# A graph network with attention on one core: the residual base moved behind a softmax, two bias rows loaded later, GpSimd given other operands in the first quad

## The chip, the core and the metric

One core of a Trainium2 chip runs the whole program. The metric is device microseconds of one execution; the time of a kernel is the median of its runs. Engines are named as the profile names them: PE (matmul), PEld (its weight loads), DVE (vector engine), ACT (scalar engine), POOL (GpSimd), SP (the engine that issues nearly all DMAs here).

## The reference

x is 1024 x 512. Sixteen graphs of 64 nodes share 16384 edges; each graph has 256 rows of conditions (`cond`, 16 x 256 x 512). All is float32.

```python
h = jnp.maximum(_layernorm(x, axis=-1), 0.0)
...
h = (h - mu) * rsqrt(var + EPS) * bn_w + bn_b
h = _gcn(h, src, dst, gcn_in_w, gcn_in_b, n)
for i in range(L):                                   # L = 4
    a = _attn(_ln(h, ln2_w[i], ln2_b[i]), cond, Wq[i], Wk[i], Wv[i], Wo[i])
    h = h + a
    u = _ln(h, ln3_w[i], ln3_b[i]) @ geglu_w[i] + geglu_b[i]
    val, gate = jnp.split(u, 2, axis=-1)
    f = val * jax.nn.gelu(gate, approximate=False)
    h = h + f @ ffo_w[i] + ffo_b[i]
h = _gcn(h, src, dst, gcn_out_w, gcn_out_b, n)
return h + x_in            # x_in is the relu above; x itself is added to the result
```

The attention has 8 heads of 64: 64 queries of a graph against its 256 conditions.

## The kernel before, in words

**Operands in parts.** [...] In the names, `ah`, `al`, `as` are the parts of a left operand, `bh`, `bl`, `bs` those of a right one, and `gr`, `gl` those of the first GEGLU weights.

**A layer.** After the queries a loop over g = 0 to 6 treats eight blocks of two graphs. In pass g PE makes keys and values of block g+1 (L370; ACT scales them out of PSUM at L381, ACT or DVE copy at L386 and L388), the scores of block g+1 (L831, in `scores`), and mixes block g (L865) and its output product (L903). DVE takes the maximum of the scores (L838), ACT the exponentials (L843), DVE the reciprocal and the scaling (L846, L848). `split_cond` splits the conditions of block g+2: high part `ah_c` on ACT (L318), low part `al_c` on DVE (L319), third part `as_c` on POOL (L324).

**The base.** What is added to the last GCN's result (x, its relu, and the bias row of the last GCN) is worked out a block of 128 rows at a time, two blocks in each layer: `fetch_x` loads x again in passes g = 1 and 2, `base_of` takes the relu on ACT (L1556), adds the bias row and the relu on DVE (L1558, L1559) and stores the sum (L1560). `load_row` (L136) loads a bias row into all 128 partitions: `bias_out` for the base, `ffb` for the feed-forward bias, which `add_bias` (L1568) adds to the rows from pass g = 6 on.

**The first GEGLU round** of a layer is written as four quads (L301 on PE), each a chain of products with sums on DVE between them (L982), the gelu on ACT (L972) and the product into `fT` (L1000, L1001). Between a quad's instructions `fill()` takes the next piece of the splitting of the seven right operands, in the order EARLY = 0, 1, 4, 6, 5, 3, 2. For an operand in BESIDE, `right_beside` has DVE make only the low halves (L1037) and POOL the third parts (L1039); for the others DVE makes both (`begin_right` L1017, `finish_right` L1025). POOL's sums for the later rounds' weights (L1081) come behind these in its order.

**Rounds 1 to 3** run as chunks (products at L1109, DVE sums at L1127 and L1144, third parts of the next chunk's weights on POOL at L1050). In the last chunk the splitting of the first rows of f (L318, L319, third part on POOL) comes in too. The output product (L1252) follows: `fr` are rows of f loaded back from DRAM (L1211), `wff` the output weights (L1220), split at L1226, L1229 and L1233.

**What sets the order.** Each engine and the SP queue take instructions in program order, which a scheduler fixes from the code's order and from contexts: `tc.issue_after(i)` places instructions behind instruction i in the order, `waiting_for(i, engine)` makes that engine's next instruction wait for i, and `in_order` and `pin` keep a given order. `scores.last` is the last scaling (L848) of the softmax that `scores` issued last.

Of the kernel before, what the change touches and what calls it, by code (L numbers as in the profile page):

```python
# [15 lines left out]
OP = mybir.AluOpType  # L16
# [5 lines left out]
TINY = 2.0 ** -12  # L22
# [4 lines left out]
def gnn_kernel(  # L27
# [26 lines left out]
    nc = tc.nc  # L54
    pin = tc.keep_in_program_order

    N, D = x.shape
# [7 lines left out]
    KC = D // P  # L65
# [4 lines left out]
    R = DFF // D  # L70
# [235 lines left out]
    def twelve_bits(t):  # L306
        return t.bitcast(F32R)
# [3 lines left out]

    def left_parts(x, name, t=None):

        parts = [slots_of(len(x), f"{n}_{name}") for n in ("ah", "al", "as")]
        for h, l, s, x in zip(*parts, x):
            nc.scalar.mul(twelve_bits(h), x, INWARD * TINY)  # L318
            nc.vector.scalar_tensor_tensor(twelve_bits(l), h, -1.0 / TINY, x, OP.mult, OP.add)  # L319
            if t:  # L320
                t.tensor_tensor(twelve_bits(s), h, l, OP.subtract)  # L321
                continue
            for k in range(2):
                nc.gpsimd.tensor_tensor(twelve_bits(s)[:, k, :], h[:, k, :], l[:, k, :],  # L324
                                        OP.subtract)
        return parts
# [678 lines left out]

    SPLIT = (0, 5, 6, 4, 1, 3, 2)
    EARLY = (0, 1, 4, 6, 5, 3, 2)
    BESIDE = (4, 6)

    def begin_right(name, x, h, s):  # L1010

# [189 lines left out]
    class Output:  # L1201
# [8 lines left out]
                self.raw[n] = slot(f"fr_{self.l}_{n}")  # L1210
                nc.sync.dma_start(self.raw[n], f_dram[s, 2 * u:2 * u + 2].rearrange("c p n -> p c n"))  # L1211

        def split(self, n, t=nc.vector):
            if n in self.raw:
                self.f[n] = left_parts([self.raw.pop(n)], f"f_{self.l}_{n}", t)

        def fetch_w(self, u):
            if u < UNITS:
# [206 lines left out]
    for l in range(L):  # L1425
# [119 lines left out]
        def fetch_x(nb):  # L1545
            if not fetched:
                fetched["bias"] = three_halves(f"bias_out_{l}")[:, :D]
                load_row(gcn_out_b, 0, "bias_out", fetched["bias"])
            fetched[nb] = acc_tile(f"x_again_{nb}")
            nc.sync.dma_start(fetched[nb], x[nb * P:(nb + 1) * P, :])  # L1550

        def base_of(nb):


            xt, bias_out, xn = fetched.pop(nb), fetched["bias"], acc_tile(f"again_{nb}")
            nc.scalar.activation(xn, xt, AF.Relu, bias=x_shift[:, nb:nb + 1],  # L1556
                                 scale=x_root[:, nb:nb + 1])
            nc.vector.tensor_tensor(xt, xt, bias_out, OP.add)  # L1558
            nc.vector.tensor_tensor(xt, xt, xn, OP.add)  # L1559
            nc.sync.dma_start(base_dram[nb], xt)  # L1560
# [2 lines left out]

        def add_bias(t, *blocks):
            if not ffb:
                ffb.append(load_row(ffo_b, l * D, f"ffb_{l}"))
            for nb in blocks:
                t.tensor_tensor(h[nb], h[nb], ffb[0], OP.add)  # L1568

# [11 lines left out]
        for g in range(NG - 1):  # L1581
# [36 lines left out]
                ln3_norm(g - 2, g - 1, behind=mix.last)  # L1618
                add_bias(nc.gpsimd, g - 2, g - 1)
            if g in (1, 2):  # L1620
                base_of(2 * l + g - 1)
            if l == 0:
                fetch_cond(g + 3)
            split_cond(l, g + 2)
# [125 lines left out]
                load()  # L1750
        sum_chunk(2)

        def split_rest(short):
            long = begin_split(0, False)
            next(long, None)
            with waiting_for(split_left.low, mybir.EngineType.Pool):
                for flow in short, long:
                    for _ in flow:
                        pass
# [4 lines left out]
        for r in range(1, R):  # L1764
            f = Gated(l, r)
            for c in range(KC):
                n = (r - R + 2) * KC + c
                if n == -1:
                    output.fetch_w(0)
                if (r, c) == (R - 1, KC - 2):  # L1770
                    output.fetch(0)
                chunk = ready.pop(0)
                flow = chunk.steps(lambda: before and sum_chunk(1))
                chunk.f = f
                next(flow)
                if 0 < n < 5:
                    next(ahead)
                for _ in islice(short, 2):
                    pass
                next(flow)  # L1780
                if before:
                    split_rest(short)
                    load()
                for _ in parts:
                    pass
                if (r, c) == (R - 1, KC - 1):
                    with in_order(mybir.EngineType.Activation), in_order(mybir.EngineType.DVE), \
                            in_order(mybir.EngineType.Pool):
                        output.split(0, nc.gpsimd)
                    output.fetch(1)  # L1790
                for step in range(3):
                    if before:
                        next(before, None)
                    next(flow)
                    if step == 1 and not before:
                        split_rest(iter(()))
                        load()
                before = flow
                short = begin_split(0, True)
                if n == 0:  # L1800
                    next(ahead)
# [153 lines left out]
```

## Time and profile before

| what | value |
|---|---|
| median of 3 runs | 2304.32 us (2302.94 to 2304.63) |
| the profiled execution | 2308.55 us |
| its span in the trace | 2306.8 us |
| PE busy | 2271.7 us, 98% |
| DVE, ACT, POOL busy | 1738.5 us (75%), 1169.6 us (51%), 750.3 us (33%) |
| granted TensorE clock, mean | 0.998 |

The rows of the timeline give the start in us, the duration in us, the engine, the line, the operation, and output<-inputs with their shapes; consecutive equal instructions are one row with a count (x4). In square brackets stands the idle time of that engine just before, and what ended it. The rows of the waits give engine, line, what was waited for, and then the total in us, the number of times, and the longest.

### The profile page before, as it was taken

The numbers are of one execution on the slowest core, as the hardware profiler recorded it, in microseconds if no ns is written. First come the engines' busy times: TensorE is split into PE (matmuls) and PEld (weight loads), VectorE is DVE, ScalarE is ACT, GpSimd is POOL, SyncE is SP. The second block draws the span as 40 slices with busy tenths as digits, with TensorE's granted clock in tenths as the row PEclk, the third lists the DMA queues.
The fourth block names the chain that finished last, engine by engine and source line by source line (L and its number), as shares of the span: only waits on it lengthen the run. The fifth ranks groups of instructions, "written<-read, shape, count | busy, mean of one in ns | idle before, by whom it ended". The sixth has DMA issues, their size and how long they took to land. (4 is left out here: it accounts for less than half of the span.)

```text
span 2306.8 us, 34462 instructions
## 1 busy us (share of the span) xinstructions
PE 2271.7 (98%) x12496; PEld 1757.1 (76%) x12496; DVE 1738.5 (75%) x3172; ACT 1169.6 (51%) x2245; POOL 750.3 (33%) x647
## 2 busy tenths in 40 slices
PE   8999999999999999999999999999999999999999
PEld 5677887587887888488787888578788788668777
DVE  9886556999986556989987554989988554899965
ACT  7555445465355445465356444556437444556521
POOL 1121213486022224377022222368112113168301
PEclk9999999999999999999999999999999999999999
DMA  7042211234512101133522111133531111043551
GB/s 214 2 151 70 69 62 36 82 119 146 183 46 74 47 28 37 60 122 96 209 91 74 38 38 38 38 109 101 192 137 51 41 47 46 1 128 110 183 171 59
DMA packets 144114, 204.42 MB, mean 89 GB/s; under 512 B 11241, under 2 KB 68913, under 8 KB 143937
## 3 DMA queue, kind: packets, MB, share of 16 engines
q1 hardware_dynamic: 141840, 196.72, 25.8%
q0 software_dynamic: 1376, 4.30, 0.6%
q8 instruction: 103, 1.69, 0.3%
q10 hardware_dynamic: 720, 1.11, 0.1%
q14 instruction: 75, 0.61, 0.1%
HBM read 151.75 MB, written 50.34 MB: 88 GB/s over the span
## 5 line engine op out<-in xcount | busy, mean ns | idle before, releaser
L324 POOL TENSOR_TENSOR as_c<-ah_c,al_c 128x512 fp32r<-128x512 f32 x128 | 200.4, 1595 | 906.6 <-DVE al_c L319 711.3
L1123 ACT ACTIVATE g<-g 128x512 f32<-128x512 f32 x192 | 112.4, 585 | 152.3 <-PE g L1109 150.7
L381 ACT ACTIVATE k<-k 128x512 f32<-128x512 f32 x125 | 73.0, 586 | 197.9 <-PE k L370 197.9
L1252 PE MATMUL fy<-bl_wff,al_f 128*128 128x512 f32 x512 | 160.1, 392 | 1.3 <-DVE bl_wff L1229 0.8
L318 ACT ACTIVATE ah_f<-fr 128x1024 fp32r<-128x1024 f32 x64 | 67.9, 1061 | 183.7 <-PE fy L1252 90.7
L1252 PE MATMUL fx<-bs_wff,as_f 128*128 128x512 f32 x512 | 160.4, 393 | 0.6 <-DVE as_f L321 0.6
L1252 PE MATMUL fy<-bh_wff,ah_f 128*128 128x512 f32 x512 | 158.4, 391 | 0.2 <-ACT ah_f L318 0.2
L386 DVE COPY kT<-k 128x512 f32<-128x512 f32 x54 | 37.2, 689 | 156.6 <-PE k L370 156.6
L370 PE MATMUL v<-bs_wv,as_c 128*128 128x512 f32 x508 | 137.4, 393 | 7.2 <-ACT v L381 7.2
L370 PE MATMUL v<-bh_wv,ah_c 128*128 128x512 f32 x508 | 141.2, 400 | 0.0
L1050 POOL TENSOR_TENSOR gsa<-gha,gla 128x512 fp32r<-128x512 f32 x96 | 124.2, 1315 | 40.2 <-DVE gla L1045 40.2
L843 ACT ACTIVATE pr<-sc,nmax 128x256 f32<-128x256 f32 x256 | 118.2, 476 | 37.3 <-DVE nmax L838 36.7
L370 PE MATMUL v<-bl_wv,al_c 128*128 128x512 f32 x508 | 136.4, 390 | 0.0
L370 PE MATMUL k<-ah_c,bh_wk 128*128 128x512 f32 x500 | 135.0, 392 | 0.0
L381 ACT ACTIVATE v<-v 128x512 f32<-128x512 f32 x127 | 75.2, 592 | 116.9 <-PE v L370 116.9
L370 PE MATMUL k<-as_c,bs_wk 128*128 128x512 f32 x500 | 132.1, 395 | 1.7 <-ACT k L381 1.7
L370 PE MATMUL k<-al_c,bl_wk 128*128 128x512 f32 x500 | 133.7, 389 | 0.0
L1109 PE MATMUL g<-gr,gha 128*128 128x512 f32 x384 | 120.0, 394 | 0.0
L1109 PE MATMUL g<-gr,gsa 128*128 128x512 f32 x384 | 120.0, 394 | 0.0
L1109 PE MATMUL g<-gl,gla 128*128 128x512 f32 x384 | 118.3, 389 | 0.0
L370 PEld LDWEIGHTS v<-bs_wv,as_c 128*128 128x128 f32 x508 | 93.1, 188 | 32.4 <-ACT v L381 10.3
L1252 PEld LDWEIGHTS fy<-bl_wff,al_f 128*128 128x128 f32 x512 | 96.3, 188 | 24.5 <-DVE bl_wff L1229 3.7
(321 smaller groups left out, 5820.7 us busy)
## 6 DMA issues: line engine op xcount, KB each, us to landing
f_dram<-fT SPq DMA_DIRECT2D x128, 256.0 KB, 2.1
fr<-f_dram SPq DMA_DIRECT2D x64, 512.0 KB, 4.3
ct<-cond_dram SPq DMA_DIRECT2D x48, 512.0 KB, 4.9
wff<-in_L_gnn_ffo_w_dram SPq DMA_DIRECT2D x32, 512.0 KB, 6.9
gxb<-in_L_gnn_geglu_w_dram SPq DMA_DIRECT2D x96, 128.0 KB, 2.5
gxa<-in_L_gnn_geglu_w_dram SPq DMA_DIRECT2D x96, 128.0 KB, 2.5
cond<-in_L_gnn_cond_dram SPq DMA_DIRECT2D x32, 256.0 KB, 3.8
cond_dram<-ct SPq DMA_DIRECT2D x16, 512.0 KB, 3.3
```

What stands on the lines that cost most here:

```text
L318: nc.scalar.mul(twelve_bits(h), x, INWARD * TINY)
L324: nc.gpsimd.tensor_tensor(twelve_bits(s)[:, k, :], h[:, k, :], l[:, k, :], OP.subtract)
L370: pin(nc.tensor.matmul(self.bank, twelve_bits(left[k // 2])[:, k % 2, self.c * P:(self.c + 1) * P], twelve_bits(right[k // 2])[:, k % 2, : ...
L381: nc.scalar.mul(self.bank, self.bank, 1.0 + TINY)
L386: nc.vector.tensor_copy(self.to(), self.bank)
L843: nc.scalar.activation(pr3[:, a, :], ps3[:, a, :], AF.Exp, bias=nmax[:, a:a + 1], accum_out=tot[:, a:a + 1])
L1050: split_left.last = pin(t.tensor_tensor(s_at, h_at, l_at, OP.subtract))
L1109: pin(nc.tensor.matmul(to, self.part(i, which)[:, k, :], self.rights[i][which].bitcast(F32R)[:, k, :], start=start and k == 0, stop=stop a ...
L1123: pin(nc.scalar.mul(to, to, 1.0 + TINY))
L1252: pin(nc.tensor.matmul(to, twelve_bits(left[which][0])[:, k, b * P:(b + 1) * P], twelve_bits(right[which])[:, k, :], start=u == 0 and whic ...
```

## The change

1. `base_of` is called under `tc.issue_after(scores.last.ins)`, so that it stands behind the softmax that was issued last.
2. The loads of `bias_out` and `ffb` wait on SP for `scores.last`, so they are made in the pass in which they are asked for.
3. BESIDE is (1, 4) in place of (4, 6).
4. In the last chunk of the last round, POOL's third parts of the weights wait for the low part of the first rows of f, and stand between it and its third part.

```diff
-    def left_parts(x, name, t=None):
+    def left_parts(x, name, t=None, between=None):
...
-            nc.vector.scalar_tensor_tensor(twelve_bits(l), h, -1.0 / TINY, x, OP.mult, OP.add)
+            left_parts.low = nc.vector.scalar_tensor_tensor(twelve_bits(l), h, -1.0 / TINY, x,
+                                                            OP.mult, OP.add)
+            if between:
+                between()
...
-    BESIDE = (4, 6)
+    BESIDE = (1, 4)
...
-                load_row(gcn_out_b, 0, "bias_out", fetched["bias"])
+                with waiting_for(scores.last, mybir.EngineType.SP):
+                    load_row(gcn_out_b, 0, "bias_out", fetched["bias"])
...
-                ffb.append(load_row(ffo_b, l * D, f"ffb_{l}"))
+                with waiting_for(scores.last, mybir.EngineType.SP):
+                    ffb.append(load_row(ffo_b, l * D, f"ffb_{l}"))
...
-                base_of(2 * l + g - 1)
+                with tc.issue_after(scores.last.ins):
+                    base_of(2 * l + g - 1)
...
-        def split_rest(short):
+        def split_rest(short, behind=None):
...
-            with waiting_for(split_left.low, mybir.EngineType.Pool):
+            with waiting_for(behind or split_left.low, mybir.EngineType.Pool):
...
                 if before:
-                    split_rest(short)
+                    if not the_last:
+                        split_rest(short)
                     load()
...
-                        output.split(0, nc.gpsimd)
+                        output.split(0, nc.gpsimd, lambda: split_rest(short, left_parts.low))
```

PE's order is the same in both kernels. Lines of the changed kernel stand 3 to 8 higher (L838 is L841, L1558 is L1562).

**The base on DVE, layer 1, pass g = 0.** `al_c_2` is the low part of block 2's conditions, `nmax_1` belongs to the softmax of block 1. Before:

```order
L319 SCALAR_TENSOR_TENSOR al_c_2_0_21145<-ah_c_2_0_21143,ct_2_0_20865 128x1024
L1558 TENSOR_TENSOR x_again_21226<-x_again_21226,bias_out_21224 128x512
L1559 TENSOR_TENSOR x_again_21226<-x_again_21226,again_21432 128x512
L319 SCALAR_TENSOR_TENSOR al_c_2_1_21146<-ah_c_2_1_21144,ct_2_1_20866 128x1024
L838 TENSOR_REDUCE nmax_1_0_21101<-sc_1_0_21081 128x2
L838 TENSOR_REDUCE nmax_1_1_21111<-sc_1_1_21082 128x2
L846 RECIPROCAL inv_1_0_21107<-tot_1_0_21104 128x2
```

After, the same place reads:

```order
L319 SCALAR_TENSOR_TENSOR al_c_2_0_21145<-ah_c_2_0_21143,ct_2_0_20865 128x1024
L319 SCALAR_TENSOR_TENSOR al_c_2_1_21146<-ah_c_2_1_21144,ct_2_1_20866 128x1024
L841 TENSOR_REDUCE nmax_1_0_21101<-sc_1_0_21081 128x2
L841 TENSOR_REDUCE nmax_1_1_21111<-sc_1_1_21082 128x2
L849 RECIPROCAL inv_1_0_21107<-tot_1_0_21104 128x2
```

The two additions are now in pass g = 1, behind the softmax of block 2:

```order
L851 TENSOR_SCALAR pr_2_3_21422<-pr_2_3_21422,inv_2_3_21426 128x256 x2
L895 SCALAR_TENSOR_TENSOR ol_1_21367<-oh_1_21366,po_1_21290 128x512
L1562 TENSOR_TENSOR x_again_21226<-x_again_21226,bias_out_21224 128x512
L896 TENSOR_TENSOR os_1_21368<-oh_1_21366,ol_1_21367 128x512
L1563 TENSOR_TENSOR x_again_21226<-x_again_21226,again_21432 128x512
L389 COPY v_2_0_21469<-v_2_1_21455 128x512
```

The second block's additions, which stood among the scalings of block 1's softmax, go behind the softmax of block 3 in the same way. On ACT the relu of the first block keeps its place; that of the second moves from the exponentials of block 1 to behind the last scaling of v in pass g = 1.

**The loads on SP, layer 0, passes g = 0 and 1.** `cond_0` to `cond_3` are raw conditions of block 3, `ct` are turned ones on their way to DRAM. Before:

```order
L1550 DMA x_again_16072<-in_x_dram 128x512
L1560 DMA base_dram<-x_again_16072 128x512
L1550 DMA x_again_16400<-in_x_dram 128x512
L270 DMA cond_0_15953<-in_L_gnn_cond_dram 128x512
L270 DMA cond_1_15954<-in_L_gnn_cond_dram 128x512
L270 DMA cond_2_15955<-in_L_gnn_cond_dram 128x512
L270 DMA cond_3_15956<-in_L_gnn_cond_dram 128x512
```

After:

```order
L1554 DMA x_again_16072<-in_x_dram 128x512
L136 DMA bias_out_16070<-in_L_gnn_gcn_out_b_dram 128x512
L270 DMA cond_0_15953<-in_L_gnn_cond_dram 128x512
L270 DMA cond_1_15954<-in_L_gnn_cond_dram 128x512
L270 DMA cond_2_15955<-in_L_gnn_cond_dram 128x512
L270 DMA cond_3_15956<-in_L_gnn_cond_dram 128x512
L276 DMA cond_dram<-ct_3_0_16040 128x1024
```

The bias row, which waits for block 1's softmax, now stands ahead of the four loads; the base's store and the second load of x have gone further down. Until now the rows of the next layer stood in the output product's start, here that of layer 0, with rows of layer 1's bias:

```order
L1193 DMA f_dram<-fT_3_1_19573 128x512 x2
L136 DMA bias_out_21224<-in_L_gnn_gcn_out_b_dram 128x512
L1211 DMA fr_1_19641<-f_dram 128x2x512
L1193 DMA f_dram<-fT_3_2_19664 128x512 x2
L1220 DMA wff_1_19704<-in_L_gnn_ffo_w_dram 128x2x512
L1220 DMA wff_2_19706<-in_L_gnn_ffo_w_dram 128x2x512
L136 DMA ffb_22720<-in_L_gnn_ffo_b_dram 128x512
L1211 DMA fr_2_19722<-f_dram 128x2x512
```

After, the two L136 rows are missing there; `bias_out` of layers 1 to 3 stands behind the loads of `ct_3`, and `ffb` ahead of the first GEGLU weights `wval` and `wgate`.

**DVE in the first quad and the start of the second, layer 0** (`gu`, `g` and `gd` with L982 are the quad's own sums, which PE waits for; `gt` is an aid of ACT's for a third part). Before:

```order
L1025 SCALAR_TENSOR_TENSOR gl_1_18319<-ln3T_0_1_17698,gr_1_18295 128x512
L982 TENSOR_TENSOR g_0_0_0_18313<-gd_0_0_18309,gu_0_0_0_18311 128x512
L1025 SCALAR_TENSOR_TENSOR gl_1_18319<-ln3T_0_1_17698,gr_1_18295 128x512
L982 TENSOR_TENSOR g_0_0_0_18312<-gc_0_0_18308,gu_0_0_0_18310 128x512
L1037 SCALAR_TENSOR_TENSOR gl_4_18331<-ln3S_0_17701,gr_4_18329 128x512
L982 TENSOR_TENSOR gd_0_0_18309<-gd_0_0_18309,gu_0_0_0_18310 128x512
L1000 SCALAR_TENSOR_TENSOR fT_0_0_18314<-ga_0_0_18125,gcols,g_0_0_0_18312 128x512
L1001 SCALAR_TENSOR_TENSOR fT_0_0_18314<-gd_0_0_18309,gcols,g_0_0_0_18313 128x512
L1037 SCALAR_TENSOR_TENSOR gl_4_18331<-ln3S_0_17701,gr_4_18329 128x512
L1037 SCALAR_TENSOR_TENSOR gl_6_18354<-ln3T_1_0_17699,gr_6_18352 128x512
L982 TENSOR_TENSOR gu_0_0_1_18372<-gb_0_1_18369,gs_0_0_0_18128 128x512
L1037 SCALAR_TENSOR_TENSOR gl_6_18354<-ln3T_1_0_17699,gr_6_18352 128x512
```

After:

```order
L1040 SCALAR_TENSOR_TENSOR gl_4_18324<-ln3S_0_17701,gr_4_18322 128x512
L985 TENSOR_TENSOR g_0_0_0_18315<-gd_0_0_18311,gu_0_0_0_18313 128x512
L1040 SCALAR_TENSOR_TENSOR gl_4_18324<-ln3S_0_17701,gr_4_18322 128x512
L985 TENSOR_TENSOR g_0_0_0_18314<-gc_0_0_18310,gu_0_0_0_18312 128x512
L1020 SCALAR_TENSOR_TENSOR gr_6_18342<-ln3T_1_0_17699,gt_6_0_18344 128x512
L985 TENSOR_TENSOR gd_0_0_18311<-gd_0_0_18311,gu_0_0_0_18312 128x512
L1003 SCALAR_TENSOR_TENSOR fT_0_0_18316<-ga_0_0_18125,gcols,g_0_0_0_18314 128x512
L1004 SCALAR_TENSOR_TENSOR fT_0_0_18316<-gd_0_0_18311,gcols,g_0_0_0_18315 128x512
L1020 SCALAR_TENSOR_TENSOR gr_6_18342<-ln3T_1_0_17699,gt_6_1_18351 128x512
L1028 SCALAR_TENSOR_TENSOR gl_6_18361<-ln3T_1_0_17699,gr_6_18341 128x512
L985 TENSOR_TENSOR gu_0_0_1_18373<-gb_0_1_18370,gs_0_0_0_18128 128x512
L1028 SCALAR_TENSOR_TENSOR gl_6_18361<-ln3T_1_0_17699,gr_6_18341 128x512
```

DVE has as many instructions as before. The four pieces that POOL follows (L1037 before, L1040 after) were those of operands 4 and 6, the last two of them in the second quad; now they are those of operands 1 (just ahead of these rows) and 4, all in the first quad, and operand 6 is DVE's alone (L1020, L1028). POOL's four third parts stand in the same place of its own order, ahead of its sums, but are those of operands 1 and 4.

More of the change, by code (lines that the diff above doesn't have):

```diff
@@ L1211, in fetch, with split @@
                 nc.sync.dma_start(self.raw[n], f_dram[s, 2 * u:2 * u + 2].rearrange("c p n -> p c n"))
-        def split(self, n, t=nc.vector):
+        def split(self, n, t=nc.vector, between=None):
             if n in self.raw:
-                self.f[n] = left_parts([self.raw.pop(n)], f"f_{self.l}_{n}", t)
+                self.f[n] = left_parts([self.raw.pop(n)], f"f_{self.l}_{n}", t, between)
         def fetch_w(self, u):
@@ L1780, in gnn_kernel @@
                 next(flow)
+                the_last = (r, c) == (R - 1, KC - 1)
                 if before:
-                    split_rest(short)
+                    if not the_last:
+                        split_rest(short)
                     load()
@@ L1785, in gnn_kernel @@
                     pass
-                if (r, c) == (R - 1, KC - 1):
+                if the_last:
                     with in_order(mybir.EngineType.Activation), in_order(mybir.EngineType.DVE), \
                             in_order(mybir.EngineType.Pool):
-                        output.split(0, nc.gpsimd)
+                        output.split(0, nc.gpsimd, lambda: split_rest(short, left_parts.low))
                     output.fetch(1)
```

## The prediction

> **What bounds the kernel now.** I read the busy shares first, then PE's waits, then the timeline around each place that the change touches.
>
> ```profile
> PE 2271.7 (98%) x12496; PEld 1757.1 (76%) x12496; DVE 1738.5 (75%) x3172; ACT 1169.6 (51%) x2245; POOL 750.3 (33%) x647
> ```
>
> PE works 2271.7 of the 2306.8 us of the span. PE's order does not change, so the change can only win or lose in the 35 us that are left. PE's waits say who holds those:
>
> ```profile
> PE v L370 <- ACT v L381: 7.2, 5, 2.2
> PE gc L301 <- DVE gu L982: 4.4, 8, 0.7
> ...
> PE g L1109 <- DVE g L1127: 1.3, 4, 0.3
> ...
> PE fy L1252 <- DVE bl_wff L1229: 0.8, 2, 0.4
> ```
>
> These four groups, 13.7 us together, lie where the edits lie; the others belong to the start and the last product. They are the most that can be won, bar the slower first matmul behind each wait. Below they are A, B, C and D.
>
> **A, the base behind the softmax.** PE, DVE, ACT and POOL in layer 1, pass g = 0:
>
> ```profile
> 720.88 0.88 PE L831 MATMUL sc<-kT,qT 64*64 64x256 f32 x12
> 729.12 1.20 PE L370 MATMUL v<-bs_wv,as_c 128*128 128x512 f32 x4 [1.52 <-ACT v L381]
> ```
> ```profile
> 718.89 0.69 DVE L1558 TENSOR_TENSOR x_again<-x_again,bias_out 128x512 f32<-128x512 f32 x1
> 719.61 1.66 DVE L1559 TENSOR_TENSOR x_again<-x_again,again 128x512 f32<-128x512 f32 x1
> 721.19 2.29 DVE L319 SCALAR_TENSOR_TENSOR al_c<-ah_c,ct 128x1024 fp32r<-128x1024 f32 x1
> 723.41 1.27 DVE L838 TENSOR_REDUCE nmax<-sc 128x2 f32<-128x512 f32 x2
> ```
> ```profile
> 719.53 1.05 ACT L318 ACTIVATE ah_c<-ct 128x1024 fp32r<-128x1024 f32 x1
> ```
> ```profile
> 719.12 3.29 POOL L324 TENSOR_TENSOR as_c<-ah_c,al_c 128x512 fp32r<-128x512 f32 x2 [18.39 <-DVE al_c L319]
> ```
>
> PE waits 1.52 us for a scaling of v that ACT reaches only behind the exponentials, which wait for the maxima. The scores begin at 720.88, but DVE takes the first maximum at 723.41, because the two additions of the base and a slow `al_c` stand ahead. The next pass has no additions there:
>
> ```profile
> 753.16 0.66 PE L831 MATMUL sc<-kT,qT 64*64 64x256 f32 x8
> 759.72 1.09 PE L370 MATMUL v<-bs_wv,as_c 128*128 128x512 f32 x4
> ```
> ```profile
> 754.29 1.29 DVE L838 TENSOR_REDUCE nmax<-sc 128x2 f32<-128x512 f32 x2 [1.45 <-PE sc L831]
> ```
> ```profile
> 758.95 0.59 ACT L381 ACTIVATE v<-v 128x512 f32<-128x512 f32 x1
> ```
>
> There the maximum comes 1.13 us behind the scores' start, the scaling ends 5.25 us behind the maximum (759.54), and PE does not wait. With the additions gone, `al_c` in layer 1 starts when `ah_c` is made, at 720.6, and takes between 1.21 (as in layer 0, below) and the 2.29 us seen beside POOL; the maximum starts between 722.0 (scores plus 1.13) and 722.9, the scaling ends between 727.3 and 728.2, and PE wants it at 729.12 - 1.52 = 727.60. Up to 0.6 us is left; I take 0.1, as POOL's pair ends by 722.4. That gains 1.4 us, and another 0.1 because four matmuls behind the wait took 1.20 us and those without it 1.09. Layer 3 has a wait of 1.52 too; the longest, 2.2, is layer 2's, of which I take 2.1. Layer 0:
>
> ```profile
> 180.60 1.05 ACT L318 ACTIVATE ah_c<-ct 128x1024 fp32r<-128x1024 f32 x1
> ```
> ```profile
> 183.51 1.21 DVE L319 SCALAR_TENSOR_TENSOR al_c<-ah_c,ct 128x1024 fp32r<-128x1024 f32 x1
> ```
> ```profile
> 189.65 1.20 PE L370 MATMUL v<-bs_wv,as_c 128*128 128x512 f32 x4 [1.69 <-ACT v L381]
> ```
>
> `al_c` can start at 181.65 and end between 182.9 and 183.9, not at 184.72, so the maximum behind it comes 0.8 to 1.9 us earlier; of the wait of 1.69 I take 1.1. Together 1.4 + 2.1 + 1.4 + 1.1 = 6.0, and 0.4 for four restarts: **6.4** (5.0 to 7.2).
>
> Where the additions go they cost 0.7 us each, or up to 1.66 beside POOL, behind a softmax whose last scaling on DVE is done, ahead of a copy of v. In that stretch DVE waits for PE for longer than this, so I take nothing, with 0 to 1 us a layer as bounds. The second relu is on ACT behind the last scaling of v, and waits for a load of x that is now issued behind the first base's store. It holds the scaling of the next keys:
>
> ```profile
> 768.24 0.58 ACT L381 ACTIVATE k<-k 128x512 f32<-128x512 f32 x1 [2.22 <-PE k L370]
> ```
> ```profile
> x_again<-in_x_dram SPq DMA_DIRECT2D x8, 256.0 KB, 4.6
> ```
>
> The adds end near 761, so a load of 4.6 us lands near 766, and a relu of 0.8 us fits before 768.24, in the 2.22 us in which ACT idles. I take nothing; a load that took 7 us would hold ACT for 1 to 2 us.
>
> **The bias rows.** In layer 0 the row of `bias_out` waits for the last scaling of block 1's softmax, near 188.7, and the four loads of `cond` stand behind it:
>
> ```profile
> 196.21 1.91 PE L205 MATMUL tr_cond<-ident,cond 128*128 128x128 f32 x16
> ```
> ```profile
> 1096.00:1104.00 8.00, 8.00 (x34) 5.88 (x33) 6.52 (x9) 3.47 (x5) 0.00 (x0) 1.00 0.88 313
> ```
> ```profile
> cond<-in_L_gnn_cond_dram SPq DMA_DIRECT2D x32, 256.0 KB, 3.8
> ...
> bias_out<-in_L_gnn_gcn_out_b_dram SPq DMA_DIRECT2D x4, 256.0 KB, 5.1
> ```
>
> The other rows give what 256 KB take from issue to landing: 5.1 us for a bias row, 3.8 for a block of `cond`. The row lands near 188.7 + 5.1 = 193.8. If it holds nothing up, the fourth load, issued near 190.5, lands 3.8 later, at 194.3; if each of the four lands some 0.7 behind the one ahead, the last comes at 196.6. (The 0.7 is an estimate from the first of these rows, the eight busy us in which the output product begins: 313 GB/s at a DMA share of 0.88 is 0.74 us for 256 KB.) PE transposes at 196.21 now and, with A's 1.1 won, wants to at 195.1. The new wait is between 0 and 1.5; I take **0.5** lost.
>
> The Trainium skill, DMA: Bandwidth & Descriptors, section Queues, rings and completion order, says that completion is not first in, first out per issuing engine. By that rule the conditions need not wait for the row, and the 0.5 would fall away; the quoted rows cannot decide it, since no load of `cond` stands behind a row in this trace.
>
> `ffb` now stands ahead of the first GEGLU weights, which POOL combines:
>
> ```profile
> 911.99 1.52 POOL L1568 TENSOR_TENSOR hall<-hall,ffb 128x512 f32<-128x512 f32 x1 [17.96 <-DVE xn_ln L193]
> ```
>
> The combining ends 17.96 us before this row. It moves later with its loads, by a row's landing and the softmax that the row waits for, some 5 to 8 us. I take nothing.
>
> **D, the output's start.** The two rows of the next layer stood there on SP ahead of `fr`:
>
> ```profile
> 1103.84 1.06 ACT L318 ACTIVATE ah_f<-fr 128x1024 fp32r<-128x1024 f32 x1 [3.73 <-DMA fr<-f_dram]
> ```
> ```profile
> 1109.47 0.50 PE L1252 MATMUL fy<-bl_wff,al_f 128*128 128x512 f32 x1 [0.40 <-DVE bl_wff L1229]
> ```
>
> ACT waits 3.73 us for `fr`, DVE's splits follow from it, and PE waits in the end. Without a row of 256 KB, and then two, the loads land 1 to 3 us earlier, more than the 0.40 that PE waits. I take all of D's 0.75 and two restarts of 0.1: **0.95** (0 to 1.1).
>
> **B, the quads.** DVE, POOL and PE in layer 1:
>
> ```profile
> 951.43 0.69 DVE L982 TENSOR_TENSOR g<-gc,gu 128x512 f32<-128x512 f32 x1 [0.43 <-PE gc L301]
> ...
> 953.14 0.70 DVE L982 TENSOR_TENSOR gd<-gd,gu 128x512 f32<-128x512 f32 x1 [0.43 <-PE gd L301]
> ...
> 956.27 0.69 DVE L982 TENSOR_TENSOR gu<-gb,gs 128x512 f32<-128x512 f32 x1
> 956.87 1.17 DVE L1037 SCALAR_TENSOR_TENSOR gl<-ln3T,gr 128x512 fp32r<-128x512 f32 x1
> 957.96 0.68 DVE L982 TENSOR_TENSOR gu<-gc,gu 128x512 f32<-128x512 f32 x1
> 958.56 1.15 DVE L1017 SCALAR_TENSOR_TENSOR gr<-ln3S,gt 128x512 fp32r<-128x512 f32 x1
> ```
> ```profile
> 955.90 4.95 POOL L1039 TENSOR_TENSOR gr<-gl,gt 128x512 fp32r<-128x512 f32 x3 [1.73 <-DVE gl L1037]
> ```
> ```profile
> 958.69 0.70 PE L301 MATMUL gc<-ln3S,wgate 128*128 128x512 f32 x1 [0.44 <-DVE gu L982]
> ```
>
> In the first quad DVE makes a sum and a piece in PE's step of 1.71 us (953.14 - 951.43) and idles 0.43 of it. In the second, beside POOL's three third parts, pieces take 1.17 and 1.15 us, DVE never idles, and PE waits 0.44 and later up to 0.7. POOL's parts move into the first quad. A pair there would take what it took beside POOL in the second: 957.96 - 956.27 = 1.69 us, just within 1.71. So the slowdown of some 0.5 us a piece falls into idle time. Quad two gets back about 0.5 us on one piece before its first wait (0.44, gone) and 0.9 on two more before its second; there POOL's sums come up instead, so of about 0.67 I take 0.4. **B gains 0.84 x 4 = 3.4** (1.0 to 4.4: the first wait with a bare margin, or both whole).
>
> **C, the last chunk.** The low part of f's rows gets free of POOL, but DVE's chain there is released by PE's own product and the product into f behind it waits for PE again. I take nothing; 0 to 1.3.
>
> **The sum.** 6.4 - 0.5 + 0.95 + 3.4 = 10.25 us. Against the profiled execution, 2308.55, that gives 2298.3. The median of the runs is 2304.32, 0.18% below the profiled one, and the same share gives **2294.1**. Within 0.2%, 4.6 us, is what a measurement of this kernel cannot tell from no change.
>
> **Rivals.**
>
> *The contention comes along.* If POOL's parts in the first quad cost PE about what they cost in the second (the margin is 1.71 against 1.69), B gives 0.5 and the sum is 7.35: 2297.0. Against it: DVE idles 0.43 in each step shown there.
>
> *A load takes the place of the wait.* Layer 0's conditions at their worst, the second relu held in ACT by a late x, and additions that hold a copy of v: 1.5 in layer 0 and 1 us in each layer, so that 10.25 + 0.5 - 1.5 - 4 = 5.25, or less with B small: 2299.1 to 2302. The same time comes out if the change does not do what it says, and the scaling of v stays late because ACT's exponentials are late by themselves: then only B and D are left, 4.3. The pass at 753 speaks against that.
>
> *POOL shuts DVE out in the first quad.* If a piece had to wait there for a whole third part of POOL's, 1.65 us long (three in 4.95), a step would be 0.60 + 0.68 + 1.65 = 2.93 us, 1.22 over PE's 1.71. Four pieces in four layers cost 19.5; the rest gains 6.85 + 4.4 = 11.3, and 8.2 is lost: 2316.8 profiled, 2312.5 on the median, slower. It decides from about 1.0 us late a piece on (16 pieces, 11.3 + 4.6). For it speaks L1559 at 1.66 against L1558's 0.69; against it the 1.17 and 1.15 above, where a piece beside these same parts lost half a microsecond.
>
> The Trainium skill, SBUF — State Buffer, section Who interferes with whom, states just such an exclusive lock: a DVE instruction with two SBUF inputs and a GpSimd one that reads SBUF, and the loser fully blocks. By that rule the last rival's time follows when POOL always comes first; the 0.5 us lost in this trace agrees with a block for a part of a POOL instruction only.
>
> **Chances.** Forecast 0.55; contention along 0.15; a load instead, or not what it says, 0.15; DVE shut out 0.10; and 0.05 for all four groups gone with C, 13.7 and restarts, near 2290. Faster by over 0.2%: the first two and the last, less a little at the edge: 0.73; within: 0.17; slower: 0.10. The range leaves out the slower rival and the lowest end: from 2289.5 (all groups gone) to 2304.5 (a load instead, with B and D at nothing as well: 2303.4, rounded up by a microsecond).
>
> **What would show it.** Right: the group v L370 <- ACT v L381 falls from 7.2 to under 1.5; the first maximum of block 1's softmax follows the scores' start by about 1.1 us; gc L301 <- DVE gu L982 falls from 4.4 to about 1; DVE's idle time in the first quad goes and L1040's pieces take about 1.2 us; fy L1252 <- DVE bl_wff is gone; PE's g L1109 <- DVE g stays at 1.3. A new wait of PE's for ct or cond in layer 0 of half a microsecond. Wrong: waits of PE's on DVE in the first quads, or of ACT on x_again with PE behind.

## The result and the profile after

The changed kernel takes **2298.87 us** (median of 13 runs, 2296.75 to 2302.24), the kernel before 2302.96 us beside it (13 runs, 2301.29 to 2305.24). The ratio is **0.9979, 95% interval 0.9972 to 0.9986**: 0.21% faster, where the prediction had 0.44% (the two medians lie 4.1 us apart, the ratio stands for 4.8). The two profiled spans lie further apart, 2306.8 and 2297.0 us; where those 9.8 us come from is told with the first experiment and at the end.

The busy time and PE's waits of the changed kernel; the groups of the prediction are A (v), B (gc), C (g L1109, now L1112) and D (bl_wff):

```profile
PE 2266.7 (99%) x12496; PEld 1756.3 (76%) x12496; DVE 1740.6 (76%) x3172; ACT 1169.7 (51%) x2245; POOL 734.3 (32%) x647
```
```profile
PE gc L301 <- DVE gu L985: 6.6, 8, 1.0
...
PE v L373 <- ACT v L384: 2.7, 5, 1.0
```

A fell from 7.2 to 2.7, not to under 1.5. C (1.3) and D (0.8) are no longer among PE's waits. **B rose from 4.4 to 6.6**, where the prediction had it fall to about 1. The first quad of layer 1 shows why, on DVE, POOL and PE:

```profile
944.25 1.37 DVE L1040 SCALAR_TENSOR_TENSOR gl<-ln3T,gr 128x512 fp32r<-128x512 f32 x1
945.54 0.68 DVE L985 TENSOR_TENSOR gu<-gc,gu 128x512 f32<-128x512 f32 x1
946.14 1.45 DVE L1040 SCALAR_TENSOR_TENSOR gl<-ln3S,gr 128x512 fp32r<-128x512 f32 x1
947.51 0.68 DVE L985 TENSOR_TENSOR g<-gd,gu 128x512 f32<-128x512 f32 x1
948.12 1.47 DVE L1040 SCALAR_TENSOR_TENSOR gl<-ln3S,gr 128x512 fp32r<-128x512 f32 x1
```
```profile
943.79 1.28 POOL L1042 TENSOR_TENSOR gr<-gl,gt 128x512 fp32r<-128x512 f32 x1 [1.32 <-DVE gl L1040]
945.76 1.28 POOL L1042 TENSOR_TENSOR gr<-gl,gt 128x512 fp32r<-128x512 f32 x1 [0.69 <-ACT gt L1037]
947.76 1.27 POOL L1042 TENSOR_TENSOR gr<-gl,gt 128x512 fp32r<-128x512 f32 x1 [0.72 <-DVE gl L1040]
```
```profile
956.52 1.98 PE L301 MATMUL gc<-ln3S,wgate 128*128 128x512 f32 x4 [0.90 <-DVE gu L985]
```

Set ends against ends. POOL's third parts end at 945.07, 947.04 and 949.03; the DVE pieces that met them end at 945.62, 947.59 and 949.59, each 0.55 us later, though the two had lain side by side for 0.82, 0.90 and 0.92 us. Elsewhere in this trace pieces of this size that found POOL at work and met it for 0.23 to 0.92 us all ended 0.55 us behind it. The piece waits for the end of POOL's instruction and then takes its own 0.68 us less 0.13. The sums between them, which read PSUM, take 0.68 beside POOL as they do alone. Since POOL's next part reads the piece, it starts 0.14 to 0.17 us after the piece has ended (ACT's `gt`, which the middle row names, ended 0.07 us behind that piece), and the two follow each other in steps of 1.97 us (946.14 to 948.12), 0.26 more than PE's 1.71. Four pieces held like this leave DVE about a microsecond late, and PE waits 0.90 where it had waited 0.44.

What is left of A in layer 1, on DVE, POOL and PE:

```profile
718.95 2.11 DVE L319 SCALAR_TENSOR_TENSOR al_c<-ah_c,ct 128x1024 fp32r<-128x1024 f32 x1 [1.64 <-ACT ah_c L318]
720.99 1.28 DVE L841 TENSOR_REDUCE nmax<-sc 128x2 f32<-128x512 f32 x2
```
```profile
717.46 2.52 POOL L327 TENSOR_TENSOR as_c<-ah_c,al_c 128x512 fp32r<-128x512 f32 x2 [18.39 <-DVE al_c L319]
```
```profile
726.41 1.20 PE L373 MATMUL v<-bs_wv,as_c 128*128 128x512 f32 x4 [0.47 <-ACT v L384]
```

The additions are gone, but `al_c` still takes 2.11 us: POOL's pair ends at 719.98, `al_c` at 721.06, again its own 1.22 less 0.14 later. The maximum comes 1.77 us behind the scores (719.22), not 1.13.

In layer 0 the bias row and the conditions behind it land late, and PE does not wait. SP, the loads' time to landing, and PE:

```profile
189.00 0.33 SPq L136 DMA_DIRECT2D bias_out<-in_L_gnn_gcn_out_b_dram  x1
189.42 1.82 SPq L270 DMA_DIRECT2D cond<-in_L_gnn_cond_dram  x4
```
```profile
DMA to landing us min/median/max: 4.7/4.9/5.1
```
```profile
195.14 1.91 PE L205 MATMUL tr_cond<-ident,cond 128*128 128x128 f32 x16
```

The four loads took 4.7 to 5.1 us behind the row (the median of all such loads in the kernel before is 3.8), so the last landed near 196: the row landed at 193.43, the loads at 194.12, 194.75, 195.40 and 196.05. PE began to turn at 195.14 without a wait: it takes one block after the other for 1.9 us, and came to the last one at 196.45, 0.4 us after that had landed.

### The profile page after: what moved, and what is told of

It is laid out like the page before. It is cut to its first block, busy times and chain, and to the rows that moved or that the text cites. A ratio compares the mean times of both kernels' runs of the same rounds, so it can differ in the third digit from the quotient of the medians.

```text
span 2297.0 us, 34496 instructions
## 1 busy us (share of the span) xinstructions
PE 2266.7 (99%) x12496; PEld 1756.3 (76%) x12496; DVE 1740.6 (76%) x3172; ACT 1169.7 (51%) x2245; POOL 734.3 (32%) x647
## 3 DMA queue, kind: packets, MB, share of 16 engines
q8 instruction: 103, 1.69, 0.3%
## 5 line engine op out<-in xcount | busy, mean ns | idle before, releaser
L1112 PE MATMUL g<-gr,gha 128*128 128x512 f32 x384 | 120.0, 394 | 0.0
L1112 PE MATMUL g<-gr,gsa 128*128 128x512 f32 x384 | 119.8, 393 | 0.0
L1112 PE MATMUL g<-gl,gla 128*128 128x512 f32 x384 | 118.2, 389 | 0.0
L373 PEld LDWEIGHTS v<-bh_wv,ah_c 128*128 128x128 f32 x508 | 93.0, 189 | 28.1 <-issue 9.2
```

The lines of the kernel that those rows point to most:

```text
L373: pin(nc.tensor.matmul(self.bank, twelve_bits(left[k // 2])[:, k % 2, self.c * P:(self.c + 1) * P], twelve_bits(right[k // 2])[:, k % 2, : ...
L1112: pin(nc.tensor.matmul(to, self.part(i, which)[:, k, :], self.rights[i][which].bitcast(F32R)[:, k, :], start=start and k == 0, stop=stop a ...
```

## The experiments

**Theory 1**: a DVE instruction that takes its data from SBUF and meets a GpSimd instruction waits until that has ended; this makes B's loss and A's remainder. **The rivals**: B's loss comes from the later loads or from ACT; A's remainder from ACT's exponentials. For sizes the table gives the time between the same two PE instructions in every trace, in us (PE's 12496 instructions have one order; the brackets give the numbers of the two, counted from 0, in the first layer concerned), summed over the layers. "Scores to output" is where A lies, "quads" B, "last chunk" C, "output" D in layers 0 to 2.

| kernel | scores to output (930 to 1000) | quads (2530 to 2660) | chunks up to the last (2660 to 3120) | last chunk (3120 to 3165) | output, layers 0 to 2 (3165 to 3300) |
|---|---|---|---|---|---|
| before | 68.7 | 197.5 | 420.8 | 46.3 | 94.3 |
| before, again | 69.0 | 197.5 | 420.9 | 46.3 | 93.3 |
| GpSimd's operands alone | 68.6 | 199.7 | 420.7 | 46.3 | 93.6 |
| base alone | 62.7 | 197.5 | 420.8 | 46.3 | 93.3 |
| changed | 62.6 | 199.6 | 420.8 | 45.2 | 91.8 |
| operands 4 and 6 again | 62.6 | 197.5 | 420.7 | 45.2 | 91.8 |
| rows loaded as before | 62.7 | 198.9 | 420.7 | 45.2 | 94.1 |
| last chunk as before | 62.7 | 200.2 | 421.0 | 46.3 | 91.8 |
| third parts behind the low parts | 63.5 | 199.4 | 420.7 | 45.2 | 91.8 |
| both mends | 63.3 | 197.4 | 420.8 | 45.2 | 91.8 |
| third parts behind the softmax, operands 4 and 6 | 59.2 | 197.5 | 420.9 | 45.2 | 91.8 |
| and none in the quads | 59.1 | 193.0 | 428.2 | 45.2 | 91.9 |
| and operands 1 and 6 | 59.3 | 200.0 | 420.8 | 45.3 | 91.8 |
| and operand 1 alone | 59.2 | 192.6 | 420.8 | 45.2 | 91.8 |

**1. The kernel before, once more.** No edit.

> The kernel before, unchanged, profiled once more. Theory 1: of the 9.8 us between the two profiled spans, about 3 us are stretches of eight matmuls at 628 ns that come and go from run to run (three in the profile of before, one in that of after), so a second profile of the same kernel should have the same waits of PE (v 7.2, gc 4.4, g 1.3, fy 0.8 us) and another number of slow stretches, with a span of 2301 to 2307 us. Rival: the slow stretches belong to the waits that the change removed, so they come back at the same three places, the one behind the wait of 2.2 us in layer 2 above all.

It took 2304.84 us, with a span of 2303.1. PE's waits:

```profile
PE v L370 <- ACT v L381: 7.4, 5, 2.5
PE gc L301 <- DVE gu L982: 4.4, 8, 0.7
```

These waits are nearly the same and the span is 3.7 us shorter. Most of the difference, 3.3 us, is slow stretches of some 3.4 us with the granted clock near a half, in which for example eight matmuls take 628 ns each. The first profile has three: at 87 us, behind the wait in layer 2, and in the output of layer 3. This one has only that in layer 2. The columns of its row are the stretch, the busy time of PE, PEld, DVE, ACT and POOL, the clock, the DMA share and GB/s:

```profile
1259.50:1263.00 3.50, 3.50 (x10) 2.69 (x10) 1.29 (x2) 0.00 (x0) 0.00 (x0) 0.51 0.00 0
```

So both the theory and its rival had a part: two of the three stretches come and go, and the third stands behind layer 2's wait in each of the three profiles with the base ahead (waits of 2.2, 2.5 and 2.1 us), and in none of the eleven with the base behind (the changed kernel's and ten below).

**2. Operands 4 and 6 again.** `BESIDE = (4, 6)` in the changed kernel.

> The changed kernel with GpSimd's third parts given back to operands 4 and 6. Theory 1: the first quads' loss is the third parts' alone: PE's waits on DVE's sums there fall from 6.6 to about 4.4 us, all else stays, the time falls by 2 to 2.5 us against the changed kernel, to a ratio of about 0.997 against before. Rival: the waits in the quads come from what the other edits moved (later loads of the bias row and the weights), so they stay at 6 us or more and the time stays at 0.998.

2297.66 us, ratio 0.9966 (0.9952 to 0.9979). PE's waits:

```profile
PE gc L301 <- DVE gu L985: 4.4, 8, 0.7
```

DVE's pieces of operand 4 take their own time again (duration min/median/max in ns):

```profile
L1040 DVE SCALAR_TENSOR_TENSOR gl<-ln3S,gr x8: 680/682/684, 420.4 to 2008.5; 128x512 fp32r<-128x512 f32 x8
```

Theory 1 holds: B is back at 4.4, and all else in the table stays. By the table this one edit of the change costs 2.1 us; in the other traces with `BESIDE = (1, 4)` the quads take 198.9 to 200.2 us, which makes it 1.4 to 2.7. The times alone do not show it: the two intervals overlap.

**3. GpSimd's operands alone.** `BESIDE = (1, 4)` in the kernel before.

> The kernel before with GpSimd's third parts moved to operands 1 and 4, nothing else. Theory 1: a DVE piece with two inputs in SBUF that meets a third part of GpSimd waits for its end; pieces in the first quad take about 1.4 us and not 0.68, PE's waits on DVE's sums rise from 4.4 to about 6.6 us, the time rises by some 2 us, ratio 1.001. Rival (that of the prediction): the pieces take 1.2 us, the waits fall to about 1 us, ratio 0.9985.

2306.04 us, ratio 1.0003 (0.9994 to 1.0013). PE's waits and DVE's pieces (duration min/median/max in ns):

```profile
PE v L370 <- ACT v L381: 7.0, 5, 2.1
PE gc L301 <- DVE gu L982: 6.7, 8, 1.0
```
```profile
L1037 DVE SCALAR_TENSOR_TENSOR gl<-ln3S,gr x8: 1440/1454/1464, 415.9 to 2012.2; 128x512 fp32r<-128x512 f32 x8
```

The pieces take 1.45 us and B is 6.7, by this edit and nothing else. The time cannot tell 2 us, the 1.001 that was expected, from none.

**4. The base alone.**

```diff
-                base_of(2 * l + g - 1)
+                with tc.issue_after(scores.last.ins):
+                    base_of(2 * l + g - 1)
```

> The kernel before with the base behind the softmax, nothing else. Theory 1: the wait for v falls from 7.2 to about 2.7 us as in the changed kernel, the quads keep 4.4, the output's start keeps its waits (0.8 us), the last chunk keeps 1.3; ratio 0.998. Rival: part of the fall of the wait for v is due to the bias row no longer being loaded early, then the wait stays above 4 us.

2299.93 us, ratio 0.9978 (0.9969 to 0.9988): as much as the whole change, in which B loses 2.1 us and C and D win 2.6 against this kernel (table). PE's waits:

```profile
PE gc L301 <- DVE gu L982: 4.4, 8, 0.7
...
PE v L370 <- ACT v L381: 2.6, 5, 1.0
...
PE g L1109 <- DVE g L1127: 1.3, 4, 0.3
```

By the table A is worth 6.0 to 6.3 us: 0.7 in layer 0, 1.0 in layers 1 and 3, and 3.3 in layer 2, of which 1.6 is the slow stretch that no longer follows. The wait for bl_wff was expected to stay and did not show here, with the rows loaded early; it comes and goes in layers 0 to 2, while the output stays longer than in the changed kernel (93.3 to 94.3 in the table, against 91.8).

**5. Third parts behind the low parts.** In the changed kernel POOL makes `as_c` of block 2 only when both `al_c` are done:

```diff
+        if late:
+            with waiting_for(left_parts.low, mybir.EngineType.Pool):
+                for h, l, s in zip(*parts):
+                    thirds(h, l, s)
...
-            conds[g] = left_parts(raw_x.pop((l, g)), f"c_{l}_{g}")
+            conds[g] = left_parts(raw_x.pop((l, g)), f"c_{l}_{g}", late=g == 2)
```

> The changed kernel in which GpSimd makes the third parts of block 2's conditions only when DVE has made both low parts of that block. Theory 1: what is left of PE's waits for v (1.0 us in layer 0, 0.47 in layers 1 to 3) is DVE's second low part, held until GpSimd's pair of third parts ends; with the pair behind it, that low part takes 1.22 us and not 2.0 to 2.1, the first maximum comes 0.8 us earlier, and PE's waits for v fall from 2.7 to about 0.4 us; the time falls by some 2.3 us, 0.1%. Rival: ACT's exponentials are late by themselves, so the low part gets shorter and the waits for v stay above 2 us.

2298.44 us, ratio 0.9969 (0.9957 to 0.9981), but PE's waits for v rose to 3.3, where a fall to 0.4 was expected. DVE and POOL in layer 1:

```profile
PE v L381 <- ACT v L392: 3.3, 5, 0.8
```
```profile
716.78 1.23 DVE L324 SCALAR_TENSOR_TENSOR al_c<-ah_c,ct 128x1024 fp32r<-128x1024 f32 x1 [1.64 <-ACT ah_c L323]
718.18 1.29 DVE L849 TENSOR_REDUCE nmax<-sc 128x2 f32<-128x512 f32 x2 [0.17 <-PE sc L842]
...
720.63 1.64 DVE L859 TENSOR_SCALAR pr<-pr,inv 128x256 f32<-128x256 f32 x2
```
```profile
718.24 5.18 POOL L318 TENSOR_TENSOR as_c<-ah_c,al_c 128x512 fp32r<-128x512 f32 x4 [21.33 <-PE sc L842]
```

The first half came as expected: `al_c` takes 1.23 us and the maximum stands 1.13 behind the scores. But POOL's four instructions now lie in the softmax, and a scaling, from SBUF to SBUF with one input, is held too (a pair took 0.60 elsewhere, 1.64 here); the last maximum behind it comes late. Theory 1 had to be widened to that scaling. In these traces a held scaling of 256 columns ends 0.15 us after POOL's instruction, a held piece of 512 columns 0.55 us after it. The Trainium skill, SBUF — State Buffer, section Who interferes with whom, has both cases: two SBUF inputs against a GpSimd instruction that reads SBUF, and `tensor_scalar` in its two-port mode; the measured rows agree that both are held, and show the mode only in that the scaling needs about half as long a column behind the wait.

**6. The rows as before.** Both `waiting_for(scores.last, mybir.EngineType.SP)` out of the changed kernel.

> The changed kernel with the two bias rows loaded where they were before. Theory 1: the output's start has its waits back, PE's wait for bl_wff of 0.7 to 0.8 us and the late weight loads behind it (0.5 us a layer in layers 0 to 2), 2 to 2.5 us in all, ratio to before 0.999 to 0.998. Rival: those waits went because the first rows of f are split earlier in the last chunk, then they stay away here and the time is that of the changed kernel.

2300.79 us, ratio 0.9979 (0.9970 to 0.9988): that of the changed kernel, where 0.998 to 0.999 was expected. This profile has no slow stretch, and that of the changed kernel has one.

```profile
PE fy L1255 <- DVE bl_wff L1232: 0.8, 2, 0.4
```

D is back, and the table has the output 2.3 us longer, 1.0 in each of layers 0 and 1, 0.3 in layer 2. So it hangs on the rows. The times alone would not show this edit.

**7. The last chunk as before.** Edit 4 out of the changed kernel.

> The changed kernel with GpSimd's third parts in the last chunk where they were before. Theory 1: the low part of f's rows takes 1.9 us again beside GpSimd, not 1.23, and PE's wait for DVE's g in the last chunk is back at 1.3 us in four waits. Rival (the prediction's reading): the wait does not hang on the low part, and stays away here for another reason.

2299.37 us (one run). PE's waits, and the low part of f in layer 1 in the kernel before and in the changed one:

```profile
PE g L1112 <- DVE g L1130: 1.3, 4, 0.3
```
```profile
1088.63 1.93 DVE L319 SCALAR_TENSOR_TENSOR al_f<-ah_f,fr 128x1024 fp32r<-128x1024 f32 x1 [0.60 <-ACT ah_f L318]
```
```profile
1086.33 1.23 DVE L319 SCALAR_TENSOR_TENSOR al_f<-ah_f,fr 128x1024 fp32r<-128x1024 f32 x1 [0.58 <-ACT ah_f L318]
```

C hangs on the low part: 1.1 us over the four layers (table).

**8. Both mends.** BESIDE = (4, 6), and experiment 5.

> The changed kernel with GpSimd's third parts in the first quads given back to operands 4 and 6, and those of block 2's conditions behind both low parts. If theory 1 holds at both places: PE's waits for v about 0.4 us, for the sums in the quads 4.4 us, for g and bl_wff none; all its waits together some 22.5 us; ratio to before 0.9955 to 0.9965, against 0.9979 of the changed kernel. If the two do not add, it stays at 0.9966, that of the first of them alone.

2296.22 us, ratio 0.9960 (0.9947 to 0.9974), with waits of 4.4 (gc) and 3.3 (v). The ratio lies where it was expected, but not for the reason given: the waits for v were to be 0.4. By the table the second mend costs 0.7 us, since it moves a stall to another place.

**9. Third parts behind the softmax.** As 8, but POOL waits for `scores.last`.

```diff
-            with waiting_for(left_parts.low, mybir.EngineType.Pool):
+            with waiting_for(late, mybir.EngineType.Pool):
...
-            conds[g] = left_parts(raw_x.pop((l, g)), f"c_{l}_{g}", late=g == 2)
+            conds[g] = left_parts(raw_x.pop((l, g)), f"c_{l}_{g}", late=scores.last if g == 2 else None)
```

> The changed kernel with GpSimd's third parts given back to operands 4 and 6 in the first quads, and those of block 2's conditions behind the whole softmax of block 1 (not only behind the low parts, where they met the scalings of that softmax). Theory 1, mended: a DVE instruction of SBUF to SBUF, the scaling with one input too, waits for the end of a GpSimd instruction; with no GpSimd instruction inside the softmax the chain takes 5.25 us from the first maximum to the end of the scaling of v, and PE's waits for v fall from 2.6 to about 0.4 us; ratio to before 0.995 to 0.996. Rival: the third parts come too late for the keys of block 2, or the chain is late for another reason, and PE waits 2 us or more there.

2293.32 us, ratio 0.9955 (0.9941 to 0.9968). PE's waits, DVE and POOL:

```profile
PE v L381 <- ACT v L392: 0.3, 1, 0.3
```
```profile
721.43 0.61 DVE L859 TENSOR_SCALAR pr<-pr,inv 128x256 f32<-128x256 f32 x2
...
725.30 1.47 DVE L904 TENSOR_TENSOR os<-oh,ol 128x512 fp32r<-128x512 f32 x1
```
```profile
724.93 5.50 POOL L318 TENSOR_TENSOR as_c<-ah_c,al_c 128x512 fp32r<-128x512 f32 x4 [27.26 <-DVE pr L859]
```

A's four waits are gone, and the third parts do not come too late for the keys. POOL now holds `os`, 1.47 and not 0.69 us, for which nobody waits. So ACT's exponentials were late here because of DVE, and not by themselves.

**10. No third parts on GpSimd in the quads.** As 9, with `BESIDE = ()`.

> The same with no third parts on GpSimd in the first quads at all: DVE makes them, four more pieces a layer. Theory 1: pieces in the first quad and up to the second's first wait take 0.68 us, PE's first wait there goes, the second falls below 0.7 us, so that PE's waits for the sums fall from 4.4 to under 2.5 us; the four more pieces end up in the last quad and the first chunk, where they cost up to 1 us a layer. Ratio between 0.9945 and 0.9965. Rival: DVE is simply full in the quads, and four more pieces make PE wait more than 4.4 us.

2295.73 us, ratio 0.9966 (0.9954 to 0.9978), at the edge of what was expected. B's wait is gone, but the price was under-estimated: the four more pieces on DVE make the chunks behind the quads 7.3 us longer (table), against 4.5 won. PE's waits show little of it:

```profile
PE g L1120 <- DVE gla L1056: 0.9, 4, 0.2
```
```profile
999.50 0.30 PEld L1120 LDWEIGHTS g<-gr,gsa 128*128 128x128 f32 x2 [0.42 <-ACT g L1134]
```
```profile
PE 2270.0 (99%) x12496; PEld 1752.5 (76%) x12496; DVE 1740.5 (76%) x3188; ACT 1169.0 (51%) x2245; POOL 720.0 (31%) x631
```

Most of it is within PE's busy time, 2270.0 us against 2264.1 in experiment 12. Four matmuls in a row take 1.07 us, 0.23 a step, while the row of one lasts 0.39: a start that is up to 0.16 late, here because a weight load waited, leaves no idle time between the rows. It shows on PEld, and in the time between two PE instructions: of the 7.3 us the chunks' waits show 1.4.

**11. Operands 1 and 6.** As 9, with `BESIDE = (1, 6)`.

> Like the first kernel of this call, but GpSimd makes the third parts of operands 1 and 6: two pieces in the first quad and two later meet it. Theory 1: 1.4 us for pieces that stand right behind one that GpSimd follows, 0.68 elsewhere; two steps of the first quad 0.26 us late, made good by the two others, so PE's waits for the sums stay at 4 to 5 us.

2296.12 us (one run); B is 6.0 us, above what was expected:

```profile
PE gc L301 <- DVE gu L993: 6.0, 8, 1.0
```

Pieces behind one that POOL follows take 1.36 to 1.46 us, the others 0.68, as foreseen. The two in the first quad are made good; the two in the second are not, since DVE has no idle time there before PE's next wait, and that was not reckoned with.

**12. Operand 1 alone.** As 9, with `BESIDE = (1,)`.

> The changed kernel with block 2's third parts behind the softmax, and GpSimd's third parts in the quads for operand 1 alone. Theory 1: its two GpSimd instructions stand in the first quad and hold two pieces there by 0.7 us each, 0.26 us over PE's step, which the steps without GpSimd (0.43 us idle each) make good before the second quad; from there to the second quad's first wait no piece meets a third part. So PE's waits for the sums in the quads fall from 4.4 us to 0.3 or less, as without any third part on GpSimd; the two pieces more on DVE cost up to half of what four cost in the first chunks (some 1.8 us a layer there). Ratio to before 0.9945 to 0.996. Rival: a late piece in the first quad is not made good, and the waits stay above 2 us.

**2288.86 us, ratio 0.9929 (0.9915 to 0.9943)**: faster than both kernels, and faster than expected (0.9945 to 0.996). DVE in the first quad of layer 1:

```profile
939.20 1.36 DVE L1048 SCALAR_TENSOR_TENSOR gl<-ln3T,gr 128x512 fp32r<-128x512 f32 x1
940.48 0.68 DVE L993 TENSOR_TENSOR gu<-gc,gu 128x512 f32<-128x512 f32 x1
941.08 1.44 DVE L1028 SCALAR_TENSOR_TENSOR gr<-ln3S,gt 128x512 fp32r<-128x512 f32 x1
...
945.46 0.70 DVE L993 TENSOR_TENSOR gd<-gd,gu 128x512 f32<-128x512 f32 x1 [0.43 <-PE gd L301]
```
```profile
PE 2264.1 (99%) x12496; PEld 1755.8 (77%) x12496; DVE 1737.5 (76%) x3180; ACT 1169.9 (51%) x2245; POOL 732.1 (32%) x639
```

Two pieces are held by 0.7 us, the first quad makes it good (DVE idles 0.43 again at its end), and no wait for the sums is left. Two more pieces on DVE cost nothing in the chunks, where some 1.8 us a layer had been allowed for; why the four of experiment 10 cost so much there and these two nothing was not looked into.

## Why the prediction was right or wrong

- **Direction and range** held: faster, and 2298.87 lies in 2289.5 to 2304.5. The size did not: 10.25 us were forecast, 4.8 measured (0.21% of 2303, interval 3.2 to 6.4 us from the ratio's). The 13 runs of each kernel told this from nothing, though the prediction had taken 0.2% as the limit of what can be told. That the time still fell into the range was in part luck: B came out 5.5 us worse than forecast, and C, D and layer 0's conditions together 2.2 to 3.2 better. It lies next to the times of the rival "A load takes the place of the wait" (2299.1 to 2302), but nothing of that rival happened.
- **A**, 6.4 forecast, 6.0 to 6.3 by the table: the size came out, by two errors that cancel. The step "I take 0.1, as POOL's pair ends by 722.4" failed: POOL's pair held `al_c` to its end, 2.11 us, and 2.4 us of waits stayed. What made up for it was not in the sum, and was luck: the slow stretch of 1.6 us behind the longest wait.
- **The conditions of layer 0**, 0.5 lost forecast, nothing lost. The loads did come in order behind the row (4.7 to 5.1 us), as at the sum's worse end; the step that failed is the taking of the last landing as PE's wait, when PE wants the last block last, 1.3 us after the first.
- **D**, 0.95 forecast, 1.5 to 2.5 by the table. The mechanism was right. Mis-sized was "D's 0.75 and two restarts of 0.1": the wait that PE shows leaves out the first 0.16 us of each late start (experiment 10), and several weight loads were late one after the other, in experiment 4 too, where that wait did not show.
- **C**, nothing forecast, 1.1. The step "DVE's chain there is released by PE's own product" was false; experiment 7 showed it hangs on the low part.
- **B**, 3.4 won forecast, **2.1 lost**. This is the step that failed: "A pair there would take what it took beside POOL in the second: 957.96 - 956.27 = 1.69 us, just within 1.71." The 1.17 us was read as a price of sharing and carried over. It is a wait for POOL's end, so its size depends on where the piece meets POOL's instruction. In the second quad of the kernel before, POOL's parts ran one behind the other, and DVE's pieces met them 0.60 to 0.62 us before their ends. In the first quad of the changed kernel each part starts just behind the piece that it reads, so the next piece meets it 0.82 to 0.92 us before its end and takes 0.7 to 0.8 us longer than alone. The other wait of each layer, which lies in the third quad and not in the second, was to shrink by 0.4; it was 0.67 to 0.68 us and is 0.48 to 1.01. The rival "POOL shuts DVE out" named the mechanism. Its step of 2.93 us was too long for the 1.97 measured: POOL's part takes 1.28 us, since the 1.65 held waits of its own, and a sum that reads PSUM runs beside it.
- **Terms taken as nothing.** The additions in their new place, the second relu and `ffb` cost nothing: from the end of "scores to output" to the quads, PE needs within 0.1 us of what it needs in the second profile of the kernel before, in every layer. One reading was not right, without harm to the sum: of PE's other waits `po` (1.2 us, four times) lies in the layers, not at the start or in the last product.

The forecast with the measured terms would be 6.2 + 2 + 1.1 - 2.1 = 7.2 us, above the interval's 6.4. The traces themselves add up: from "before, again" to "changed" the table's columns win 7.0 us, a slow stretch at 125 us, which the profile of the changed kernel has and most others lack, takes back 1.7, small differences along the execution give 0.7, and the spans differ by 6.0. What separates 7.2 from the 4.8 of the runs stays open. Slow stretches come and go, and the medians of the kernel before alone lie between 2302.96 and 2306.21 us in the five groups of runs. Its first profiled execution took 2308.55 us, 5.6 above the median of the 13 runs.

## What to carry to other kernels

An instruction that takes longer beside another engine's may be waiting for that engine's end, as every held piece here did: compare the two ends before carrying the figure to another place. Work on GpSimd that follows a DVE piece holds the next DVE piece, so in a case like this put it where DVE reads PSUM, or where DVE idles, and give it no more than the idle time makes good. An edit that moves a stall out of one chain should be checked for the chain it lands in, as the scalings showed.

## What the runs showed of the hardware

- In layer 2, waits of PE of 2.1 to 2.5 us were followed by some 3.4 us (eight matmuls) at about half the clock in three profiles of three, and waits of 1.5 us at the same place in layers 1 and 3 in none. The length alone does not decide it: of twelve waits of 1.85 to 2.13 us in the first 130 us of the fourteen profiles, four were followed by such a stretch. The Trainium skill, TensorE: Matmul & The Clock Gate, section HAM oscillation — how this bites in real kernels, gives as its rule no gaps of PE above some 3.4 us; here such stretches came behind shorter ones. They also came where three waits of 0.2 to 0.6 us lay close together, in the output of layer 3 in three profiles of fourteen.
- PE's waits leave out the first 0.16 us of each late start, since a matmul's row lasts 0.39 us where the next one can begin after 0.23. Of the 7.3 us of experiment 10 the four chunks' waits show 1.4.
- A DVE instruction that was held beside GpSimd ended a fixed time after GpSimd's: 0.55 us for 128x512 with two inputs from SBUF, 1.08 for 128x1024, 0.15 for a scaling of 128x256.
